# The scan's last product of each state, made by ScalarE and added to y by an accumulating DMA

## The chip, the cores and the metric

The kernel runs on one core of a Trainium2 chip. The metric is the device time in microseconds of one execution; a kernel is compared by the median of its runs. Engines are named as in the profile: PE is TensorE (matrix products and transposes; PEld its weight loads), DVE is VectorE, ACT is ScalarE, POOL is GpSimd, SP is SyncE, which here only issues DMAs.

## The reference

Two layers on x of shape 4 x 64 x 64 x 256, all in float32. The first is a state-space block with a convolution and a feed-forward part, the second is attention over the 4096 pixels of an image. What matters here is the scan in the first layer. Windows of 2 x 2 pixels are sequences of four steps; each of 384 channels has eight states:

```python
dt = silu(dt_raw @ dt_W + dt_b)
dA = exp(dt[..., None] * -exp(A_log))
dBx = dt[..., None] * b_st[:, :, None, :] * x[..., None]
def step(state, inp):
    dA_t, dBx_t, c_t = inp
    state = dA_t * state + dBx_t
    y = einsum('bcn,bn->bc', state, c_t)
    return state, y
...
y_ssm = 0.5 * (y_fwd + y_bwd)          # the scan forwards and backwards over the window
y = alpha * y_ssm + (1 - alpha) * gelu(depthwise_conv(x_proj) @ pw_W)
x_out = x + (y * silu(z)) @ out_W
out1 = x_out + gelu(layernorm(x_out) @ W1 + b1) @ W2 + b2
# second layer: softmax(g f^T) h, times Wo and gamma, plus its input
```

So y at each of the four steps is a sum of eight products, a state times its c, from each direction.

## The kernel before

The first layer goes through 32 blocks (four images, eight blocks each) of 512 pixels. A block's 512 pixels are 128 windows on the partitions times four steps t. Channels-first tiles are [128, 3, 512], and tiles with the windows on the partitions, such as u (dt times x) and y, are [128, 4, 384]: step t, then channels. The second layer, attention, handles 128 queries at a time beside the first layer's later blocks, and 256 queries at a time once the first layer is done.

`scan` handles one block. y starts at t = 0 and 3 with a product by ACT (L438) and one by DVE (L440). Then 25 rounds j follow, in which the forward direction (d = 0) does step j and the backward direction (d = 1) does step j - 1. A step is a pair of state n and position k (j = 3n + k, k = 0, 1, 2), and has these parts:

- `decays` (L406): three ACT exponentials for a direction and state, one state ahead, into a tile e of which there are three.
- `turned` (L462): three PE transposes of a 128-column piece of e into one PSUM bank.
- `decayed` (L470, L474): DVE multiplies the bank with the state before, giving p.
- `carried` (L492): for k < 2, DVE adds the new input to p, giving the state h.
- `given` (L485, or L483 on ACT for two first writes in a block): c times the state is added to y at step t = order[d][k + 1]. For k < 2 the state is h. For k = 2, the last step of the direction, there is no `carried`, and the state is p. For k = 2, t is 3 for d = 0 and 0 for d = 1; no other step of the scan touches y at t = 0 or 3 after L440.

After the scan, `merge` (L562 to L564) transposes y with PE, in the order f, then t = 0, 1, 2, 3, into a bank, and DVE adds it, scaled, to the block's xc.

The program is written as generators, and each engine executes its instructions in the order in which they are written out. A `yield` carries an estimated cost. `first_layer` alternates a block's scan with the pieces of the block before's convolution and `tail` and of the next block's `head` in proportion to these costs. `ensue` puts the next block's `prepare` near the scan's end. Between scan and merge come the rest of the next head's pieces and the next block's `inputs(at + 1, 0)` (L419 to L423). In attention, `fill(RATE)` takes 5.7 cost units of the first layer per step of `attend`.

`layernorm` (L295 to L303), called twice in a block, has DVE statistics, then two small POOL instructions, ve (L300) and rstd (L301), and then four DVE instructions (L303) that need rstd. POOL otherwise adds a bias row (L660), and clears edges (L534, L546) and a column of ones (L700). POOL issues no DMA in this kernel; loads and stores are issued by SP, weights by ACT.

`SLOTS` lists tiles whose memory the late attention uses for its exponentials, and `quarter` loads an image's keys into a tile; `late_weights` calls it for an image that no earlier call has loaded.

Of the kernel before, what the change touches and what calls it, by code (L numbers as in the profile page):

```python
# [21 lines left out]
F32 = mybir.dt.float32  # L22
# [6 lines left out]
P = 128  # L29
DIM = 256  # L30
INNER = 384
# [28 lines left out]
def block_then_attention_kernel(  # L60
# [366 lines left out]
    def scan(at, ensue):  # L427

        bc, cb, dts, es = steps[at]
        if at == 0:  # L430
            yield from inputs(at, 0)
        yield from inputs(at, 1)
        decays(at, 0, 1)
        u = us[at, 0], us[at, 1]
        y = one.tile([P, 4, INNER], F32, tag="y", name="y")

        for t in (0, 3):
            nc.scalar.activation(y[:, t, :], u[0][:, t, :], AF.Copy, scale=cb[:, 2 * t : 2 * t + 1])  # L438
        for t in (0, 3):
            nc.vector.scalar_tensor_tensor(  # L440
                y[:, t, :], u[1][:, t, :], cb[:, 2 * t + 1 : 2 * t + 2], y[:, t, :], ALU.mult, ALU.add
            )
        yield 1.1

        order = ((0, 1, 2, 3), (3, 2, 1, 0))
        hs = {}

        def place(d, j):  # L450

            if at < NBLK and (2 * j + d) % 4 == 3:
                return pso.tile([P, TOK], F32, tag="pso", name="pa")
            return bank()

        def turned(d, j):

            n, k = divmod(j, 3)
            off = (order[d][k + 1] - (1 - d)) * P
            pa = place(d, j)  # L460
            for f in range(KI):
                nc.tensor.transpose(pa[:, f * P : (f + 1) * P], es[d, n][:, f, off : off + P], ident)  # L462
            return pa

        def decayed(d, j, pa):
            n, k = divmod(j, 3)
            t0 = order[d][k]
            p = three.tile([P, INNER], F32, tag="p", name="p")
            if k == 0:
                nc.vector.scalar_tensor_tensor(  # L470
                    p, pa[:, :INNER], bc[:, t0, d, n : n + 1], u[d][:, t0, :], ALU.mult, ALU.mult
                )
            else:
                nc.vector.tensor_tensor(p, pa[:, :INNER], hs[d], ALU.mult)  # L474
            return p

        def given(d, j, p):
            n, k = divmod(j, 3)
            t = order[d][k + 1]
            h = hs[d] if k < 2 else p  # L480
            c = bc[:, t, d, NST + n : NST + n + 1]
            if d == 0 and n == 0 and k < 2:
                nc.scalar.activation(y[:, t, :], h, AF.Copy, scale=c)  # L483
            else:
                nc.vector.scalar_tensor_tensor(y[:, t, :], h, c, y[:, t, :], ALU.mult, ALU.add)  # L485

        def carried(d, j, p):
            n, k = divmod(j, 3)
            if k < 2:
                t = order[d][k + 1]  # L490
                hs[d] = three.tile([P, INNER], F32, tag="h", name="h")
                nc.vector.scalar_tensor_tensor(  # L492
                    hs[d], u[d][:, t, :], bc[:, t, d, n : n + 1], p, ALU.mult, ALU.add
                )


        pas = {(0, 0): turned(0, 0)}
        for j in range(3 * NST + 1):
            n, k = divmod(j, 3)
            first, second = j < 3 * NST, j > 0  # L500
            if k == 2 and n + 1 < NST:
                decays(at, n + 1, 1)
            if first and k == 1 and n + 1 < NST:
                decays(at, n + 1, 0)
            p0 = decayed(0, j, pas.pop((0, j))) if first else None
            p1 = decayed(1, j - 1, pas.pop((1, j - 1))) if second else None
            if first:
                carried(0, j, p0)
                if j + 1 < 3 * NST:
                    pas[0, j + 1] = turned(0, j + 1)  # L510
                pas[1, j] = turned(1, j)
                yield 1.3
            if second:
                carried(1, j - 1, p1)
            if first:
                given(0, j, p0)
            if second:
                given(1, j - 1, p1)
            yield 2.0
            if j == 3 * NST - 4:  # L520
                ensue = ensue()
            if j >= 3 * NST - 4:
                for cost in ensue:
                    yield cost
                    if j < 3 * NST and cost > 2.0:
                        break
        merged[at] = y
# [27 lines left out]
    def merge(at):  # L555

        y = merged.pop(at)
        xc = heads[at][1]
        for f in range(KI):
            py = bank()  # L560
            for t in range(4):
                nc.tensor.transpose(py[:, t * P : (t + 1) * P], y[:, t, f * P : (f + 1) * P], ident)  # L562
            nc.scalar.activation(xc[:, f, :], xc[:, f, :], AF.Copy, scale=half_d[:, f : f + 1])
            nc.vector.scalar_tensor_tensor(xc[:, f, :], py, half_a[:, f : f + 1], xc[:, f, :], ALU.mult, ALU.add)  # L564
            yield 1.1
# [237 lines left out]
    def quarter(b, pool, tag):  # L803

        fQ = pool.tile([P, N // 4], F32, tag=tag, name="fQ")
        for i in range(NBLK):
            nc.sync.dma_start(
                out=fQ[CK * (i % 4) : CK * (i % 4 + 1), (i // 4) * TOK : (i // 4 + 1) * TOK],
                in_=fgd[b * NBLK + i][:CK, :],
            )  # L810
        quarters[b] = fQ
# [81 lines left out]
    def until(at):  # L893
# [2 lines left out]


    SLOTS = (
        (three, "xc"), (three, "e"), (two, "u"), (two, "dt"), (one, "y"), (one, "yz"), (three, "xc"), (three, "e"),
        (three, "xc"), (three, "e"), (two, "u"), (two, "dt"), (two, "xnT"), (two, "xnT"), (one, "ff"), (one, "zs"),  # L900
    )

# [20 lines left out]
    def late_weights(b, q, odd, es):  # L923


        if b not in quarters:
            quarter(b, one, "norm" if b % 2 else "xo")
        fQ, gq = quarters[b], gqs.pop((b, q))
        mx = two.tile([P, 2, QB], F32, tag="uT", name="mx")
        for g in range(4):  # L930
            pr = four()
            for s in range(2):
                at = (g // 2) * TOK + (2 * (g % 2) + s) * P
                for r in range(4):
                    nc.tensor.matmul(  # L935
                        pr[r][:, s * QB : (s + 1) * QB], lhsT=fQ[CK * r : CK * (r + 1), at : at + P],
                        rhs=gq[CK * r : CK * (r + 1), :], start=True, stop=True,
                    )
            for a in range(2):
                pool, tag = SLOTS[8 * odd + 2 * g + a]  # L940
                e = pool.tile([P, 2, 2, QB], F32, tag=tag, name="eT")
                for j in range(2):
                    nc.scalar.copy(e[:, j], pr[2 * a + j].rearrange("p (s q) -> p s q", s=2))  # L943
                if g == 0 and a == 0:
                    nc.vector.tensor_tensor(mx, e[:, 0], e[:, 1], ALU.max)
                else:
                    for j in range(2):
                        nc.vector.tensor_tensor(mx, mx, e[:, j], ALU.max)  # L948
                es.append(e)
                yield  # L950
        yield
        yield
        both = one.tile([P, 2, QB], F32, tag="mx", name="m2")
        m2, nb = both[:, 0, :], both[:, 1, :]
        nc.vector.tensor_tensor(m2, mx[:, 0, :], mx[:, 1, :], ALU.max)
        pm = aside()
        for c in range(2):
            nc.tensor.transpose(pm[:, c * P : (c + 1) * P], m2[:, c * P : (c + 1) * P], ident)
        nm = st.tile([P, 2], F32, tag="nm", name="nm")
        nc.vector.tensor_reduce(  # L960
            nm, pm[:, :QB].rearrange("p (c k) -> p c k", c=2), AX.X, ALU.max, negate=True
        )
        wide = three.tile([P, 2, P], F32, tag="p", name="nmb")
        for c in range(2):
            nc.vector.tensor_copy(wide[:, c, :], nm[:, c : c + 1].to_broadcast([P, P]))
        yield
        pn = aside()
        for c in range(2):
            nc.tensor.transpose(pn[:, c * P : (c + 1) * P], wide[:, c, :], ident)
        nc.scalar.copy(nb, pn[:, :QB])  # L970
        for n, e in enumerate(es):
            e4 = e.rearrange("p r s q -> p (r s) q")
            nc.vector.tensor_tensor(e4, e4, nb.unsqueeze(1).broadcast_to([P, 4, QB]), ALU.add)
            nc.scalar.activation(e, e, AF.Exp)
            if n % 2:
                yield
# [213 lines left out]
```

## Time and profile before

| | |
|---|---|
| median of 3 runs | 5246.53 us (5246.45 to 5246.89) |
| profiled execution, span from first to last instruction | 5245.1 us; the page gives it no other time, and the median lies 1.4 us above |
| instructions | 77394 |
| ACT busy | 3582.8 us, 68% |
| POOL busy | 208.3 us, 4% |
| DMA | 592.13 MB, mean 113 GB/s |
| mean granted PE clock | 0.972 |

Busy times are the sums of an engine's instruction times, overlaps counted once. In a row of the groups, the two numbers after the bar are the busy time of the group in microseconds and the mean duration of one instruction in nanoseconds; after the second bar stands the time that the engine was idle just before these instructions, and what ended it. A row of the waits has the waiting instruction, what it waited for, and then the total in microseconds, the number of times and the longest wait. Matmuls are pipelined, so a group's durations overlap, and the distance between starts tells the cost of one.

### The profile page before, as it was taken

The numbers are of one execution on the slowest core, as the hardware profiler recorded it, in microseconds if no ns is written. First come the engines' busy times: TensorE is split into PE (matmuls) and PEld (weight loads), VectorE is DVE, ScalarE is ACT, GpSimd is POOL, SyncE is SP. The second block draws the span as 40 slices with busy tenths as digits, with TensorE's granted clock in tenths as the row PEclk, the third lists the DMA queues.
The fourth block names the chain that finished last, engine by engine and source line by source line (L and its number), as shares of the span: only waits on it lengthen the run. The fifth ranks groups of instructions, "written<-read, shape, count | busy, mean of one in ns | idle before, by whom it ended". The sixth has DMA issues, their size and how long they took to land. (4 is left out here: it accounts for less than half of the span.)

```text
span 5245.1 us, 77394 instructions
## 1 busy us (share of the span) xinstructions
PE 4861.3 (93%) x27444; PEld 3509.2 (67%) x27444; DVE 4585.4 (87%) x8391; ACT 3582.8 (68%) x5508; POOL 208.3 (4%) x304
## 2 busy tenths in 40 slices
PE   7999998899999999999899999999999889899999
PEld 4565565666666666666666666666666666678887
DVE  7999999889989989988999988899889898866665
ACT  6778778667776767766676766777676767455554
POOL 0000000000000000000000000000000000000000
PEclk8999999999999999999999999999999999999999
DMA  1010011344444434444434444444444344344444
GB/s 48 26 44 19 23 34 36 119 127 126 135 128 135 129 122 122 131 127 124 134 119 127 131 124 127 122 134 128 130 131 131 115 129 130 121 146 147 148 146 139
DMA packets 355779, 592.13 MB, mean 113 GB/s; under 512 B 55104, under 2 KB 95296, under 8 KB 355392
## 3 DMA queue, kind: packets, MB, share of 16 engines
q1 hardware_dynamic: 351872, 583.31, 36.7%
q8 instruction: 217, 3.56, 0.3%
q10 hardware_dynamic: 3520, 3.87, 0.2%
q14 instruction: 170, 1.39, 0.1%
HBM read 528.18 MB, written 58.79 MB: 112 GB/s over the span
## 5 line engine op out<-in xcount | busy, mean ns | idle before, releaser
L1039 PE MATMUL acc<-vt,eq 128*128 128x257 f32 x5888 | 1521.2, 394 | 41.3 <-issue 19.3
L1039 PEld LDWEIGHTS acc<-vt,eq 128*128 128x128 f32 x5888 | 1090.2, 196 | 296.9 <-issue 130.7
L406 ACT ACTIVATE e<-dt,a_sc 128x384 f32<-128x384 f32 x1536 | 853.0, 611 | 250.0 <-PE bank L462 239.7
L462 PE MATMUL bank<-ident,e 128*128 128x128 f32 x4320 | 662.1, 280 | 105.9 <-DVE p L474 59.1
L462 PEld LDWEIGHTS bank<-ident,e 128*128 128x128 f32 x4320 | 523.4, 143 | 329.4 <-issue 94.3
L492 DVE SCALAR_TENSOR_TENSOR h<-u,bc,p 128x384 f32<-128x384 f32 x1024 | 613.1, 611 | 0.1
L852 ACT COPY eq<-q 128x512 f32<-128x512 f32 x736 | 386.1, 588 | 306.7 <-PE q L844 191.4
L485 DVE SCALAR_TENSOR_TENSOR y<-h,bc,y 128x384 f32<-128x384 f32 x960 | 589.4, 614 | 3.6 <-ACT y L483 1.3
L474 DVE TENSOR_TENSOR p<-bank,h 128x384 f32<-128x384 f32 x960 | 515.5, 547 | 49.1 <-PE bank L462 48.4
L878 ACT ACTIVATE eq<-eq 128x1024 f32<-128x1024 f32 x368 | 383.2, 1052 | 145.1 <-DVE eq L877 142.7
L877 DVE TENSOR_TENSOR eq<-eq,nb 128x1024 f32<-128x1024 f32 x368 | 443.6, 1217 | 23.0 <-ACT nb L873 22.6
L595 DVE SCALAR_TENSOR_TENSOR ydw<-xp,vec,ydw 128x512 f32<-128x512 f32 x640 | 462.8, 742 | 0.4
L1014 PE MATMUL bank<-vt,eT 128*128 128x257 f32 x1728 | 432.3, 382 | 0.0
L860 DVE TENSOR_TENSOR mx<-mx,eq 128x512 f32<-128x512 f32 x552 | 382.5, 693 | 52.7 <-ACT eq L852 45.2
L1014 PEld LDWEIGHTS bank<-vt,eT 128*128 128x128 f32 x1728 | 323.4, 189 | 55.6 <-issue 8.6
L485 DVE SCALAR_TENSOR_TENSOR y<-p,bc,y 128x384 f32<-128x384 f32 x512 | 314.0, 613 | 0.1
L626 PE MATMUL q<-ydw,wpw 128*128 128x512 f32 x576 | 282.8, 625 | 30.9 <-ACT eq L852 18.1
L470 DVE SCALAR_TENSOR_TENSOR p<-bank,bc,u 128x384 f32<-128x384 f32 x480 | 291.5, 607 | 17.4 <-PE bank L462 17.0
L406 ACT ACT_TABLE_LOAD x225 | 288.7, 1283 | 10.8 <-PE bank L462 7.0
L844 PE MATMUL q<-gq,fQ 32*128 32x128 f32 x5888 | 246.8, 293 | 35.5 <-ACT eq L852 17.5
L844 PEld LDWEIGHTS q<-gq,fQ 32*128 32x128 f32 x5888 | 202.6, 194 | 105.4 <-ACT eq L852 26.9
L948 DVE TENSOR_TENSOR mx<-mx,eT 128x512 f32<-128x512 f32 x252 | 174.4, 692 | 95.5 <-ACT eT L943 74.8
(153 smaller groups left out, 7021.0 us busy)
## 6 DMA issues: line engine op xcount, KB each, us to landing
vt<-vod SPq DMA_DIRECT2D x1760, 257.0 KB, 2.8
vod<-vst SPq DMA_DIRECT2D x32, 514.0 KB, 4.1
xt<-in_x_dram SPq DMA_DIRECT2D x256, 64.0 KB, 1.9
xo<-in_x_dram SPq DMA_DIRECT2D x256, 64.0 KB, 2.6
x1d<-xo SPq DMA_DIRECT2D x32, 512.0 KB, 2.9
res<-x1d SPq DMA_DIRECT2D x92, 128.0 KB, 2.8
out_dram<-res SPq DMA_DIRECT2D x368, 32.0 KB, 1.6
fgd<-fg SPq DMA_DIRECT2D x32, 256.0 KB, 2.1
```

What stands on the lines that cost most here:

```text
L406: nc.scalar.activation(e[:, f, :], dts[d][:, f, lo : lo + 3 * P], AF.Exp, scale=a_sc[:, d, f * NST + n : f * NST + n + 1],)
L462: nc.tensor.transpose(pa[:, f * P : (f + 1) * P], es[d, n][:, f, off : off + P], ident)
L474: nc.vector.tensor_tensor(p, pa[:, :INNER], hs[d], ALU.mult)
L485: nc.vector.scalar_tensor_tensor(y[:, t, :], h, c, y[:, t, :], ALU.mult, ALU.add)
L492: nc.vector.scalar_tensor_tensor(hs[d], u[d][:, t, :], bc[:, t, d, n : n + 1], p, ALU.mult, ALU.add)
L595: nc.vector.scalar_tensor_tensor(o, x_tap, w_tap, o, ALU.mult, ALU.add)
L844: ins = nc.tensor.matmul(pr[r][:, s * P : (s + 1) * P], lhsT=fQ[CK * r : CK * (r + 1), at : at + P], rhs=gq[CK * r : CK * (r + 1), :], sta ...
L852: nc.scalar.copy(e[:, j, :], pr[2 * a + j])
L877: nc.vector.tensor_tensor(e8, e8, nb.unsqueeze(1).broadcast_to([P, 8, P]), ALU.add)
L878: nc.scalar.activation(e, e, AF.Exp)
L1014: nc.tensor.matmul(sums[c][:, : DIM + 1], lhsT=e[:, r % 2, s, c * P : (c + 1) * P], rhs=vt[:, s, :], start=(n == 0 and s == 0), stop=(n == ...
L1039: nc.tensor.matmul(acc[:, : DIM + 1], lhsT=es[k // 2][:, k % 2, a : a + P], rhs=vt[:, s, :], start=(n == 0 and s == 0), stop=(n == 2 * NI ...
```

## The change

For k = 2, `given` no longer uses DVE. ACT multiplies p by c into a new tile q (128 x 384, of which there are two), and a DMA issued by POOL adds q to y at step t in SBUF. y becomes four tiles, one for each t, where it was one tile; the other uses of y are rewritten for that. The late attention uses the memory of the tile xo where it used y's, and `quarter` always uses the memory tag "norm" for an image that late attention loads.

```diff
-        y = one.tile([P, 4, INNER], F32, tag="y", name="y")
+        y = [one.tile([P, INNER], F32, tag=f"y{t}", name=f"y{t}") for t in range(4)]
...
             c = bc[:, t, d, NST + n : NST + n + 1]
-            if d == 0 and n == 0 and k < 2:
-                nc.scalar.activation(y[:, t, :], h, AF.Copy, scale=c)
+            if k == 2:
+                q = two.tile([P, INNER], F32, tag="q", name="q")
+                nc.scalar.activation(q, h, AF.Copy, scale=c)
+                nc.gpsimd.dma_start(out=y[t], in_=q, accum_op=ALU.add)
+            elif d == 0 and n == 0:
+                nc.scalar.activation(y[t], h, AF.Copy, scale=c)
             else:
-                nc.vector.scalar_tensor_tensor(y[:, t, :], h, c, y[:, t, :], ALU.mult, ALU.add)
+                nc.vector.scalar_tensor_tensor(y[t], h, c, y[t], ALU.mult, ALU.add)
...
-                nc.tensor.transpose(py[:, t * P : (t + 1) * P], y[:, t, f * P : (f + 1) * P], ident)
+                nc.tensor.transpose(py[:, t * P : (t + 1) * P], y[t][:, f * P : (f + 1) * P], ident)
...
-        (three, "xc"), (three, "e"), (two, "u"), (two, "dt"), (one, "y"), (one, "yz"), (three, "xc"), (three, "e"),
+        (three, "xc"), (three, "e"), (two, "u"), (two, "dt"), (one, "xo"), (one, "yz"), (three, "xc"), (three, "e"),
...
-            quarter(b, one, "norm" if b % 2 else "xo")
+            quarter(b, one, "norm")
```

More of the change, by code (lines that the diff above doesn't have):

```diff
@@ L434, in scan @@
         u = us[at, 0], us[at, 1]
-        y = one.tile([P, 4, INNER], F32, tag="y", name="y")
+        y = [one.tile([P, INNER], F32, tag=f"y{t}", name=f"y{t}") for t in range(4)]
         for t in (0, 3):
-            nc.scalar.activation(y[:, t, :], u[0][:, t, :], AF.Copy, scale=cb[:, 2 * t : 2 * t + 1])
+            nc.scalar.activation(y[t], u[0][:, t, :], AF.Copy, scale=cb[:, 2 * t : 2 * t + 1])
         for t in (0, 3):
             nc.vector.scalar_tensor_tensor(
-                y[:, t, :], u[1][:, t, :], cb[:, 2 * t + 1 : 2 * t + 2], y[:, t, :], ALU.mult, ALU.add
+                y[t], u[1][:, t, :], cb[:, 2 * t + 1 : 2 * t + 2], y[t], ALU.mult, ALU.add
             )
```

## The prediction

> **What bounds the kernel now.** I read the page's busy times first, then the windows, because one average hides three stages: scan and convolution blocks alone (to about 920 us), the same blocks beside attention (to about 4540), attention alone.
>
> ```profile
> PE 4861.3 (93%) x27444; PEld 3509.2 (67%) x27444; DVE 4585.4 (87%) x8391; ACT 3582.8 (68%) x5508; POOL 208.3 (4%) x304
> ```
>
> The busy time by stage, in windows that leave out the seams (columns: length, then busy us and instruction count per engine, granted clock, DMA share, GB/s):
>
> ```profile
> 122.00:786.00 664.00, 632.86 (x2771) 392.40 (x2770) 648.51 (x1310) 514.54 (x823) 43.42 (x64) 0.99 0.09 29
> 931.00:4540.00 3609.00, 3316.63 (x19764) 2428.26 (x19763) 3257.03 (x5950) 2536.11 (x3881) 147.05 (x209) 0.97 0.42 127
> 4600.00:5245.00 645.00, 637.36 (x3687) 518.45 (x3685) 401.11 (x573) 316.52 (x464) 0.11 (x1) 1.00 0.49 146
> ```
>
> In the first stage DVE is busy 648.5 of 664 us (98%): it is the bound. One block takes 94.8 us, the distance of one merge (L562) from the next. In the mixed stage PE and DVE are both near 90%, a block takes about 160 us, and neither is the bound alone. The last stage has no scan: nothing happens to it.
>
> What DVE waits for in the mixed stage (us in total, times, longest):
>
> ```profile
> DVE mx L858 <- ACT eq L852: 48.5, 25, 3.6
> DVE p L474 <- PE bank L462: 48.4, 37, 3.7
> DVE mx L860 <- ACT eq L852: 45.2, 32, 4.5
> DVE xt L303 <- POOL rstd L301: 28.8, 20, 1.5
> ```
>
> It waits on PE, ACT and POOL in turns, so a DVE instruction taken away is not given back whole there. PE busy counts pipelined ends; the last chain piece runs 128 matmuls of 257 columns in 27.78 us, 0.844 ns a column. Summing the columns of the matmul records at that pitch (row-packed ones shared out), PE needs about 0.90 of the first stage and 0.83 of the mixed one. So there is room behind DVE, but little in the first stage.
>
> **What is removed.** The groups:
>
> ```profile
> L485 DVE SCALAR_TENSOR_TENSOR y<-p,bc,y 128x384 f32<-128x384 f32 x512 | 314.0, 613 | 0.1
> L483 ACT ACTIVATE y<-h,bc 128x384 f32<-128x384 f32 x64 | 39.2, 613 | 31.0 <-DVE h L492 30.8
> L301 POOL TENSOR_TENSOR rstd<-ve,mhalf 128x4 f32<-128x4 f32 x64 | 67.9, 1061 | 5.3
> L300 POOL TENSOR_SCALAR ve<-mv 128x4 f32<-128x4 f32 x64 | 26.3, 410 | 3566.8 <-DVE mv L297 3401.2 <-DVE rg L983 165.6
> ```
>
> The first row is exactly what goes: 32 blocks x 8 states x 2 directions = 512. Their cost to DVE is the pitch, not the 613 ns, because starts overlap ends (DVE timeline; start, duration):
>
> ```profile
> 441.24 0.61 DVE L485 SCALAR_TENSOR_TENSOR y<-p,bc,y 128x384 f32<-128x384 f32 x1
> 441.76 0.61 DVE L485 SCALAR_TENSOR_TENSOR y<-h,bc,y 128x384 f32<-128x384 f32 x1
> 442.29 0.61 DVE L470 SCALAR_TENSOR_TENSOR p<-bank,bc,u 128x384 f32<-128x384 f32 x1
> ```
>
> So 0.527 us each: 512 x 0.527 = 270 us, 8.4 us a block; 67 in the first eight blocks, 202 in the other 24. How much reaches the end lies between nothing and all. First stage: per 94.8 us DVE falls from 92.9 to 84.5, below PE's 85; the floor is then PE and I take half, 34 us. Mixed stage: DVE falls from 90% to 85%, level with PE's 83% (0.97 clock); I take half, 101. Gain 135.
>
> **What is added on ACT.** 512 scaled copies of L483's form: 613 ns, pitch 0.51, so 261 us; ACT goes from 77% to 86% in the first stage and from 70% to 75.5% in the mixed one. It is off the path where ACT runs ahead; where it is late, PE and DVE already wait (DVE 115 us on ACT's eq and nb copies, PE about 70, in the mixed stage). I raise those 185 by 5.4/70: 14 us. Behind the waiting copy in ACT's queue stand exponentials and attention's evacuations. In 217 places (seven per block) I compared the end of the exponentials that will stand ahead of the copy with the start of the L485 it replaces: ACT is ahead in 120, by 1.9 us on the mean of all, and late in 97, by 0.87. Waiting while ahead costs nothing unless PE is already short of banks; cover gone, 1.9 x 512 = 970 us of waiting at most, of which I take none.
>
> **What is added on POOL and the queues.** 512 DMA issues stand in POOL's queue, each waiting for ACT's copy and for the accumulate before it into the same y. The trace has no DMA issued from POOL. Its time on POOL: 0.1 us (a small memset) to 1.75 (the largest POOL instruction, L272); I take 1.06, the rstd row. Landing, from the DMA rows (KB, median us):
>
> ```profile
> vt<-vod SPq DMA_DIRECT2D x1760, 257.0 KB, 2.8
> vod<-vst SPq DMA_DIRECT2D x32, 514.0 KB, 4.1
> ```
>
> out_dram's 32 KB takes 1.6; with 192 KB I take 2.8, ends 1.6 and 4.1. The path is SBUF to SBUF with an add, which no row has. From the time L485 could start: 0.87 + 0.61 + 1.06 + 2.8 = 5.34 us. Nothing in the scan reads y[0] or y[3] between steps, and accumulates into one tile are three steps (over 10 us) apart, so order and the two q buffers cost nothing; without that gap each step would wait a landing. None of these additions can be a gain. SP's queue is passed by nothing. The DMA engines gain 101 MB, some 17% on 592; at 42% busy the vt loads, issued four ahead, hide it.
>
> The Trainium skill, "SBUF — State Buffer", section "Who interferes with whom", speaks against this: a DMA issued from GpSimd has its descriptors written by GpSimd, which cannot do so while VectorE runs a two-port mode; it names 620 ns growing to 3100. In this trace the scan's DVE instructions take 547 to 613 ns for 384 elements, over one cycle each at the page "VectorE: DVE Perf Modes"'s 0.96 GHz, and only L589 (512 elements, 478 ns, 80 times) looks faster. By the page's worst case, an estimate, each landing would come 2.5 us later, the merges would wait 41 us more by the sums below, and the time would be 5208; by the trace's rows it is the 5167 below, which I keep.
>
> **Where it is waited for.** (1) merge transposes y[0] first. Last L485 of a block, and the merge:
>
> ```profile
> 403.22 0.60 DVE L485 SCALAR_TENSOR_TENSOR y<-p,bc,y 128x384 f32<-128x384 f32 x1
> ```
> ```profile
> 406.85 1.63 PE L562 MATMUL bank<-ident,y 128*128 128x128 f32 x12
> ```
>
> That is 3.6 us in six of the first eight blocks, and 0.7 to 9.6 in the others. Summing what 5.34 exceeds it by: 13.6 us in the first eight, 36.7 in the rest. Behind PE's wait stand the convolution and attention matmuls. I count the first in full, the second half: 32. (2) layernorm's ve and rstd queue behind a DMA on POOL, and DVE waits for rstd in order. The distance from the start of the latest y<-p to ve is under 0.87 + 0.61 + 1.06 = 2.54 us in 7 of 64 layernorms; summing what it lacks: 9. With 1.75 us on POOL, (1) and (2) give 42 and 15.
>
> The y split, the SLOTS name and quarter's tag cost nothing: only batch 3 calls quarter late, with "norm" already, and xo's last readers end before late attention starts.
>
> Sum: -135 + 14 + 32 + 9 = -80 against the span 5245.1; the runs' median lies 1.4 above it. 5246.5 - 80 = 5166.5, say 5167.
>
> **Rivals.** *POOL's issue is slow (slower).* Place: POOL's in-order queue; if one issue holds POOL 4.5 us, ve waits about 80 us over the 64 layernorms (64 at 4 us, 97 at 5), the first merges 41 and half of the other merges' 101, with ACT's 14 that is 186 against 135: 5297. It decides from about 3.5 us (the same sums give 114 at 3, 160 at 4). For it: nothing in the trace bounds a POOL-issued DMA; against it: rows up to 1.75. *The saved DVE time is not on the path (no change).* A fifth of 270 returns, 54, against 55 added: 5246. For it: PE's 0.90 and the mixed waits; against it: DVE's 98% and PE's own waits for DVE p at L462, 76 us in the mixed stage. *More than half returns.* Three quarters, 202, less 40: 5085.
>
> **How the numbers follow.** A measurement tells about 0.2%, 10 us, from no change. Forecast, with the third rival on its side: 0.59 faster (0.49 and 0.10). No change 0.08. POOL slow, and any dearer landing: 0.33. Both signs hold much, so the range runs 5085 to 5300; the forecast's own is 5110 to 5220.
>
> **What would show it.** DVE busy down by about 300 (314 less overlaps), L485 only 960, ACT up by about 310, block distance near 90.5 in the first stage and near 157 in the mixed one, PE waiting for a DMA on y ahead of L562 about 50 us. I am wrong if rstd waits at L303 grow from 60 us towards 150, if POOL's DMA rows exceed 3.5 us, or if DVE's idle grows by all that was removed.

## The result

The changed kernel takes 5262.44 us (median of 6 runs, 5251.62 to 5271.21) beside 5246.49 us for the kernel before: a ratio of 1.0029, 95% interval 1.0018 to 1.0041. It is 16 us slower, where 80 us faster was forecast. The profiled execution, with a span of 5249.8 us, is the fastest of the six, which follow the granted clock (5251.6 us at 0.975, 5271.2 at 0.970), so its trace shows less of the loss, 4.7 us, than the medians do.

The work moved as the change says. The busy times on the page after:

```profile
PE 4854.9 (92%) x27444; PEld 3511.3 (67%) x27444; DVE 4356.6 (83%) x7879; ACT 3821.6 (73%) x6011; POOL 649.4 (12%) x816
```

DVE has 512 instructions and 229 us less, ACT 239 us more, POOL 441 us more. The same windows as before the change, first stage and mixed stage:

```profile
122.00:786.00 664.00, 628.50 (x2732) 388.48 (x2731) 589.93 (x1188) 554.22 (x916) 139.44 (x174) 0.99 0.29 62
931.00:4540.00 3609.00, 3311.59 (x19773) 2428.64 (x19772) 3096.51 (x5584) 2716.99 (x4250) 458.55 (x571) 0.97 0.55 147
```

In the first stage DVE falls from 648.5 to 589.9 us of 664, 98% to 89%, and PE from 632.9 to 628.5: neither of the two is busier (ACT is, 554.2 us for 514.5), and yet a block takes 96.6 us from merge to merge, not 94.8. In the mixed stage a block takes 159.0 us (159.2 before; mean of 23). DVE's time was taken away, and DVE idles instead. What it waits for in the whole run:

```profile
DVE p L474 <- PE bank L462: 89.5, 59, 5.5
DVE mx L864 <- ACT eq L856: 70.6, 51, 3.8
DVE xc L568 <- PE bank L566: 55.3, 23, 5.0
DVE xt L303 <- POOL rstd L301: 46.7, 32, 1.5
```

The first two are waits of before that grew (L474, and L860 there). The third is merge (L564 before, 4.8 us then). The new work itself, in the groups and the DMA issues:

```profile
L484 ACT ACTIVATE q<-p,bc 128x384 f32<-128x384 f32 x512 | 308.9, 609 | 114.2 <-DVE p L474 64.6 <-issue 41.5 <-ACT e L406 5.5
L485 POOL DMA_DIRECT2D y<-q x512 | 445.6, 890 | 3262.7 <-ACT q L484 2925.1 <-PE acc L1043 84.8 <-ACT xp L540 49.6
```
```profile
y<-q POOLq DMA_DIRECT2D x512, 192.0 KB, 3.5
```

One issue holds POOL 0.89 us on the mean, and the data has landed 3.5 us after the issue began (median). Now the end of one first-stage block, engine by engine (start, duration): DVE's last p, ACT up to its last copy, POOL's last issue, PE's transposes of y, DVE's merge.

```profile
399.41 0.55 DVE L474 TENSOR_TENSOR p<-pa,h 128x384 f32<-128x384 f32 x1
```
```profile
399.69 0.61 ACT L406 ACTIVATE e<-dt,a_sc 128x384 f32<-128x384 f32 x1
400.32 1.28 ACT L346 ACT_TABLE_LOAD   x1
401.62 0.69 ACT L346 ACTIVATE zs<-q,b_in 128x512 f32<-128x512 f32 x1
402.32 1.28 ACT L406 ACT_TABLE_LOAD   x1
403.62 0.61 ACT L406 ACTIVATE e<-dt,a_sc 128x384 f32<-128x384 f32 x1
404.14 0.60 ACT L484 ACTIVATE q<-p,bc 128x384 f32<-128x384 f32 x1
```
```profile
405.03 0.86 POOL L485 DMA_DIRECT2D y<-q  x1 [5.51 <-ACT q L484]
```
```profile
408.12 1.50 PE L566 MATMUL bank<-ident,y 128*128 128x128 f32 x12 [0.84 <-DMA y<-q]
```
```profile
408.79 2.07 DVE L568 SCALAR_TENSOR_TENSOR xc<-bank,half_a,xc 128x512 f32<-128x512 f32 x3 [4.92 <-PE bank L566]
```

The last p was ready at 399.96, but ACT came to its copy only 4.2 us later: two exponentials, a silu of the gate (L346) and the two table loads around it stood ahead. PE reaches merge 8.2 us after p, where before it took 3.6 us from the start of the last L485. PE itself idles only 0.84 us, because fourteen convolution matmuls were put ahead. DVE idles 4.92 us, and about as long in five of the six middle blocks of the stage.

### The profile page after: what moved, and what is told of

Read it like the earlier page. It is cut to its first block, busy times and chain, and to the rows that moved or that the text cites. A ratio compares the mean times of both kernels' runs of the same rounds, so it can differ in the third digit from the quotient of the medians.

```text
span 5249.8 us, 78912 instructions
## 1 busy us (share of the span) xinstructions
PE 4854.9 (92%) x27444; PEld 3511.3 (67%) x27444; DVE 4356.6 (83%) x7879; ACT 3821.6 (73%) x6011; POOL 649.4 (12%) x816
## 3 DMA queue, kind: packets, MB, share of 16 engines
q1 hardware_dynamic: 351872, 583.31, 36.8%
q0 software_dynamic: 73728, 100.70, 11.9%
## 5 line engine op out<-in xcount | busy, mean ns | idle before, releaser
L485 POOL DMA_DIRECT2D y<-q x512 | 445.6, 890 | 3262.7 <-ACT q L484 2925.1
L474 DVE TENSOR_TENSOR p<-bank,h 128x384 f32<-128x384 f32 x960 | 519.6, 553 | 91.6 <-PE bank L462 89.5
L484 ACT ACTIVATE q<-p,bc 128x384 f32<-128x384 f32 x512 | 308.9, 609 | 114.2 <-DVE p L474 64.6
L630 PE MATMUL q<-ydw,wpw 128*128 128x512 f32 x576 | 273.0, 608 | 34.5 <-ACT eq L856 28.3
```

What stands on the lines that cost most here:

```text
L485: nc.gpsimd.dma_start(out=y[t], in_=q, accum_op=ALU.add)
```

## Experiments

Each run is compared with runs of the kernel before made beside it: median 5245.08 us for e1 to e4, 5240.58 for e5 to e8, 5239.22 for e9 to e12. Differences below are against these. Theory W was: the gain is there, and waits at a block's end eat it. Its rival P: the gain was never there.

**e1: only the split of y.**

```diff
-            if k == 2:
-                q = two.tile([P, INNER], F32, tag="q", name="q")
-                nc.scalar.activation(q, h, AF.Copy, scale=c)
-                nc.gpsimd.dma_start(out=y[t], in_=q, accum_op=ALU.add)
-            elif d == 0 and n == 0:
+            if d == 0 and n == 0 and k < 2:
```

> y in four tiles and the late tags moved, and the scan's last product on DVE as before. Theory W (the gain is eaten by new waits at a block's end: ACT's copy late, DMA landing, DVE held at merge): 5246, within 5. Theory P (DVE's time isn't what the span is made of; PE with its weight loads and the order of work set it): also about 5246. Theory O (every edit makes the engines' orders anew, and that alone moves the time): off by 10 to 30 us either way.

Measured 5244.12 us, ratio 1.0 (0.999 to 1.0009). The four tiles and the late attention's tags cost nothing. Theory O is not tested by this run, although it was meant to be: every edit lets the planner order the engines' instructions anew, but here PE's, DVE's and POOL's orders came out the same as before in every place, by the names in the trace.

**e2: the product left out.**

```diff
             if k == 2:
-                q = two.tile([P, INNER], F32, tag="q", name="q")
-                nc.scalar.activation(q, h, AF.Copy, scale=c)
-                nc.gpsimd.dma_start(out=y[t], in_=q, accum_op=ALU.add)
+                pass
```

> The last product of each direction (512 products) is left out altogether: no DVE, no ACT, no DMA for it. This is what 270 us of DVE time are worth with nothing put in their place. W: 5246 - 135 = 5111 (5070 to 5150), the first stage's block from 94.8 to about 90.5 us. P: 5225 to 5250, the block near 94 us.

Measured 5166.67 us, ratio 0.9852 (0.9837 to 0.9866): 78 us. So both theories miss: the gain that could be had is neither 135 nor nothing. Most of it, 67 us in the traces, lies in the mixed stage, where a block falls from 159.2 to 156.2 us: 2.9 of the 8.4 us that were taken from DVE. The first stage's block stays at 94.6. The window of its six middle blocks (columns as above), before and in this run:

```profile
218.00:784.00 566.00, 541.23 (x2372) 334.82 (x2372) 553.36 (x1118) 439.33 (x704) 37.26 (x55) 1.00 0.09 28
```
```profile
218.00:784.00 566.00, 541.09 (x2372) 336.00 (x2371) 514.21 (x1028) 440.43 (x707) 37.27 (x56) 0.99 0.09 28
```

DVE is busy 39 us less and every other engine does the same work in the same time. The first block is different: its merge comes 8.4 us earlier than before (113.3 for 121.7 us), all that was taken from DVE there. In its scan PE had room, being busy 61 of 76 us, where DVE was busy 72 (the kernel before):

```profile
44.00:120.00 76.00, 60.91 (x227) 33.85 (x227) 72.07 (x143) 51.84 (x84) 0.00 (x0) 0.77 0.03 8
```

**e3: ACT's copies, without the DMA** (q is added to nothing).

```diff
                 nc.scalar.activation(q, h, AF.Copy, scale=c)
-                nc.gpsimd.dma_start(out=y[t], in_=q, accum_op=ALU.add)
```

> ACT makes q as in the changed kernel, but q is added to nothing: no DMA. W: 14 us above the run that leaves the product out altogether, so 5125 (5085 to 5165). P, with ACT as the cause: within 10 of the changed kernel, 5250 to 5265. The difference to the run without ACT's copies is ACT's price, the difference to the changed kernel is the DMA's.

Measured 5200.51 us, ratio 0.9917 (0.9902 to 0.9932): 45 us below before, so ACT's copies cost 34 us, not 14, and the DMA the other 61 (to 16 above). A block is 95.6 us in the first stage and 157.1 in the mixed one, 1.0 and 0.9 above e2. In this trace the clock granted in the first stage's middle blocks was 0.98, in e2's 0.99, so the 1.0 is not cleanly ACT's.

**e4: the last state on DVE.**

```diff
-            if k == 2:
+            if k == 2 and n + 1 < NST:
...
-            elif d == 0 and n == 0:
+            elif d == 0 and n == 0 and k < 2:
```

> As the changed kernel, but the last state's product (n = 7) of both directions stays on DVE, so nothing that merge waits for comes by DMA late: 448 products by ACT and DMA, 64 on DVE. W: DVE's wait of about 5 us at merge in the first stage goes, and half of the others': 5190 to 5215. P: 5250 to 5262, like the changed kernel.

Measured 5229.55 us, ratio 0.9968 (0.9957 to 0.9979). With the complete result it beats both kernels: 15.5 us below before, 31 below the changed kernel. It lies between the two theories, which e2 explains: the gain W counted on is smaller. DVE's wait at merge:

```profile
L568 DVE SCALAR_TENSOR_TENSOR xc<-bank,half_a,xc 128x512 f32<-128x512 f32 x96 | 67.8, 747 | 5.6 <-PE bank L566 5.2
```

**e5: the product left out, and three taps of the first stage's convolution from PE to DVE** (ACT loses its copy of that channel group with them, 0.59 us a block).

```diff
-        yield from depthwise(ydw, (9, 9, 0) if b == 0 else (0, 0, 0))
+        yield from depthwise(ydw, (9, 6, 0) if b == 0 else (0, 0, 0))
```

> The product left out altogether as in e2 (5166.7), and in the first stage three of the second channel group's nine convolution taps moved from PE to DVE: PE has 2.6 us less a block, DVE 2.0 more. Theory P1 (in the first stage PE is the bound, although DVE is busy 98% there before): the first stage's block falls from 94.6 to about 92.5, 5150 to 5158. Theory S (a chain of waits through all engines sets the block): 94 to 96, 5160 to 5175.

Measured 5137.75 us, ratio 0.9801 (0.9786 to 0.9816): 103 us below before, 24 more than e2. The first stage's block falls to 92.2 us, by 2.4 of the 2.6 us taken from PE, although DVE got 2.0 more:

```profile
218.00:784.00 566.00, 539.24 (x2392) 337.43 (x2391) 535.67 (x1070) 454.74 (x719) 37.56 (x56) 0.99 0.09 28
```

With DVE relieved, PE sets the first stage. By the traces 15 us of the gain over e2 lie there; another 9 came in the mixed stage, whose work is that of e2 but whose granted clock was 0.978, not 0.972.

**e6: the last state's accumulates into a tile of their own** (y lacks these).

```diff
+    aside_y = wp.tile([P, INNER], F32, name="aside_y")
+    nc.gpsimd.memset(aside_y, 0.0)
...
-                nc.gpsimd.dma_start(out=y[t], in_=q, accum_op=ALU.add)
+                nc.gpsimd.dma_start(out=y[t] if n + 1 < NST else aside_y, in_=q, accum_op=ALU.add)
```

> ACT and DMA work exactly as in the changed kernel, but the last state's 64 accumulates go into a tile of their own that nobody reads (so y lacks these), and merge waits for no late DMA. Theory W (the landing that merge waits for is the larger part of the DMA's 62 us): 5262 - 38 = 5224 (5215 to 5232). Theory C (the DMAs cost by POOL's time, the port or the traffic, wherever they land): 5250 to 5262.

Measured 5208.72 us, ratio 0.9937 (0.9922 to 0.9952): 32 below before, where the changed kernel is 16 above. ACT, POOL and DMA work is the same (but for one small memset), so what merge waits for is 48 us. The other DMAs, with their 448 issues and landings, cost 13 us over e3, within the two intervals; PE's order is the same in e3 and in this run.

**e7: ACT's copies made from u instead of p** (and added to nothing).

```diff
-                nc.scalar.activation(q, h, AF.Copy, scale=c)
-                nc.gpsimd.dma_start(out=y[t], in_=q, accum_op=ALU.add)
+                nc.scalar.activation(q, u[d][:, t, :], AF.Copy, scale=c)
```

> ACT's 512 copies as in e3 (5200.5), but made from u, which is long there, in place of p, and added to nothing. Theory B (ACT's price of 34 us is its occupancy, 0.51 us each): 5193 to 5205. Theory F (the price is ACT waiting for p, and what stands behind it): 5167 to 5180.

Measured 5207.08 us, ratio 0.9934 (0.9917 to 0.995): not faster than e3. ACT idled 108.5 us ahead of its copies in e3 and 0.3 us here, so its price is not the wait for p but the time of the copies among ACT's other work. The traces show where that time is waited for: PE's waits that ended on ACT add up to 138 us in e2, 172 in e3 and 187 here, and most of the growth is behind attention's emptying of a PSUM tile (PE q <- ACT eq: 78, 102 and 108).

**e8: e4 only from block 8 on.**

```diff
-            if k == 2:
+            if k == 2 and n + 1 < NST and at >= NBLK:
...
-            elif d == 0 and n == 0:
+            elif d == 0 and n == 0 and k < 2:
```

> As e4 (last state on DVE; 5229.6), and only from block 8 on; the first eight blocks as before. The complete result. Theory P1 (in the first stage the saved DVE time is worth nothing, and ACT and DMA cost 0.8 us a block there): 5219 to 5225. If the first stage's change did help: 5230 to 5240.

Measured 5228.05 us, ratio 0.9976 (0.9967 to 0.9986), 12.5 below before; e4 was 15.5 below. The first stage's block is 94.7 us again (95.6 in e4), but the mixed one is 158.5 (158.2), and no difference remains that these intervals can tell.

**e9: the kernel before, with the taps moved alone** (the edit of e5).

> The kernel before with only the three taps moved from PE to DVE in the first stage (2.6 us less on PE, 2.0 more on DVE a block). If PE alone is the bound there: the block falls from 94.8 to about 92.5, 5222 to 5230. If both PE and DVE bind, which e2 and e5 together suggest: the block rises to 95.5 to 97, 5245 to 5260.

Measured 5260.80 us, ratio 1.0042 (1.0027 to 1.0057): 22 us slower, a block 96.6 us, 1.8 longer for 2.0 us more on DVE.

```profile
218.00:784.00 566.00, 529.72 (x2293) 327.11 (x2291) 551.87 (x1111) 425.65 (x684) 37.28 (x55) 0.98 0.09 28
```

So in the first stage of before DVE, busy 97.5% here, sets the block as well: more DVE work lengthens it at nearly the full price, and less DVE work doesn't shorten it (e2). The two bound it at almost the same length. That less PE work helps only once DVE has room fits this run but isn't shown by it alone: at a granted clock of 0.98, where before had 1.00, PE was busy 90.9 us a block, as long as before (90.6). By the traces 12 of the 22 us came up to the eighth merge; the rest came later, where the work is that of before.

**e10: e4 with the taps moved** (the edits of e4 and e5).

> e4 (last state's product on DVE, the other 448 by ACT and DMA) with the three taps moved as in e5. The complete result. Both bind in the first stage: e4's 0.9968 of the kernel before less about 27 us, 5195 to 5212, the first stage's block near 93. ACT or POOL binds there by now: 5222 to 5235.

Measured 5210.72 us, ratio 0.9946 (0.9932 to 0.9961): with the complete result the best of all, 28.5 us below before. The first stage's block is 93.3 us, as expected; the mixed one is 158.8, 0.6 above e4's, which keeps the sum at the upper end.

**e11: the last state at high priority in the planner.**

```diff
-                nc.scalar.activation(q, h, AF.Copy, scale=c)
-                nc.gpsimd.dma_start(out=y[t], in_=q, accum_op=ALU.add)
+                with tc.high_priority() if n + 1 == NST else nullcontext():
+                    nc.scalar.activation(q, h, AF.Copy, scale=c)
+                    nc.gpsimd.dma_start(out=y[t], in_=q, accum_op=ALU.add)
```

> The changed kernel with the last state's copies and accumulates at high priority in the planner that orders the engines' work. The complete result. Theory W (ACT reaches the last copy 4.2 us late in the first stage, 1.7 in the mixed one, and DVE waits for what follows at merge): DVE's wait at merge falls from 54 to about 20 us, 5230 to 5245. If ACT's place is not moved by it: 5255 to 5265.

Measured 5247.54 us, ratio 1.0009 (0.9999 to 1.002). ACT now reaches the last copy 0.9 us after p in the first eight blocks (4.2 in the changed kernel) and 0.6 in the others (1.7). DVE's idle time at merge (L569) is 34.5 us, not 20:

```profile
L569 DVE SCALAR_TENSOR_TENSOR xc<-bank,half_a,xc 128x512 f32<-128x512 f32 x96 | 67.4, 745 | 34.5 <-PE bank L567 34.0
```

The first stage's block falls to 95.1, but the mixed one is 159.5. An earlier place in ACT's order takes away 21 of the 55 us of DVE's wait; what stays, against 5.6 in e4, goes with the copy, the issue and the landing. The whole run is 8 us above before, the changed kernel 16, and the two intervals touch.

**e12: e2 with less PE work in the mixed stage** (one of three partial products of the pointwise convolution left out from block 8 on, beside e2's product).

```diff
+            nk = KI if b == 0 else KI - 1
-            for k in range(KI):
+            for k in range(nk):
...
-                    start=(k == 0), stop=(k == KI - 1),
+                    start=(k == 0), stop=(k == nk - 1),
```

> The product left out as in e2, and from block 8 on one of the three partial products of the pointwise convolution is left out too: PE has 2.6 us less a block there, 61 us in all, and nothing else changes. If PE binds the mixed stage for the part that DVE doesn't (DVE gave back 3.0 of 8.4 us a block): 30 to 45 us below e2. If PE is no bound there: within 8 of e2 (0.985 of the kernel before).

Measured 5113.37 us, ratio 0.976 (0.9745 to 0.9775): 126 below before, 47.5 more than e2, for 61 us of PE time: 78% comes back, against 29% of DVE's 270 in e2 (2.9 of 8.4 us a block in the mixed stage alone). With DVE relieved, PE is what most of the mixed stage is made of. A little of it may be the clock (0.975 granted in the mixed stage, 0.972 in e2), and no run took PE work away there with DVE's left as before.

## Why the prediction was wrong

Its sum was -135 + 14 + 32 + 9 = -80. The runs give -78 (e2), +34 (e3 less e2), +48 (changed kernel less e6) and +13 (e6 less e3): +17. But for rounding they must add up to the measured 16, as each is the difference to the next run. Of the 97 us between the two sums, 57 are gain that did not come, 20 are ACT's, 16 merge's and 4 the last term's.

**The step that failed first is "I take half".** The count of 512 and the pitch of 0.527 us were right, and so was the note that part of 270 us is not given back. But the first stage was read as "DVE is busy 98%: it is the bound", with PE's need put at 0.90 by its pitch, and 34 us were counted there. e2 shows 11.5 by the eighth merge, 8.4 of them in the first block, and next to nothing in the middle ones: 94.8 to 94.6. PE's busy time in that window, 541 of 566 us in both runs, was the sign that I argued away as pipelined ends; e5 shows that it was real. In the mixed stage 101 was taken and 67 came. What stands in its place is PE (e5, e12). The traces agree: PE's waits that ended on DVE add up to 222 us in the kernel before and to 143 in e2, a fall of 79 beside a gain of 78 (its waits on ACT rose by 19, its busy time fell by 21). The 222 stood in the trace ahead of the change, against the 270 that the sum started from.

**ACT's 14 was 34.** I scaled the waits that already ended on ACT by its added share. This leaves out that a copy of 0.51 us also delays the evacuations behind it that PE waits for: PE's waits that ended on ACT grew by 35 us from e2 to e3. DVE's waits for ACT, most of what I had scaled, are no measure of it. The two mx rows (L858 and L860 before) add up to 94 us before, to 121 in e2, where ACT makes no copies, and to 128 in e3, so most of their growth comes with the relieved DVE and not with ACT's copies.

**Merge's 32 was 48, and fell on another engine.** The landing was put 5.34 us after p; it is 8.3 us in the first eight blocks and 7.3 in the others, means over all blocks, until PE's transposes. Issue and landing were about right: 1.06 + 2.8 = 3.86 us were put, and from the start of a block's last issue to its landing it is 3.1 us in the first eight blocks and 4.1 in the others. The largest miss is ACT's lag behind p: 0.87 was put, and at a block's end it is 4.2 us in the first eight blocks and 1.7 in the others. In the block shown above, a silu of the gate with its two table loads is most of it. The 0.87 was a mean over 217 steps, seven in a block; over the other 480 copies of the changed kernel the lag is 2.0 us on the mean and 0.9 at the median. I expected PE to wait "about 50 us"; PE's own waits for the DMA are 29.7 us, and DVE's idle time at merge is 55.3.

**The 9 us for rstd were about nothing.** DVE's waits at L303 rose from 60.4 to 74.3 us, but in e2, where POOL issues no DMA, they are 72.1: it is the relieved DVE that comes earlier. e6's 13 us for all DMAs but the last stand in its place, little above the runs' spread.

**The rivals.** "The saved DVE time is not on the path" was the nearest: 54 of gain against 55 of cost, where it was 78 against 95. Of the signs of being wrong the last one came: DVE's busy time fell by 229 us and its idle time grew by 234. The slow rival had its mechanism wrong: POOL's issue is 0.89 us, far under the 3.5 from which it was to decide. The Trainium skill, "SBUF — State Buffer", section "Who interferes with whom", would have a POOL issue wait while VectorE runs a two-port instruction. No run here shows a delay like the one that the prediction priced at 2.5 us: the median of 512 issues is 859 ns and the longest 1245, with DVE busy 83% of the span. The 42 issues that overlap a TENSOR_SCALAR of DVE (L303, or L593, the L589 of before) have a median of 923 ns, the other 470 of 859.

A statement ahead of the prediction is wrong, too: instructions are not issued in the order in which they are written out. The planner orders each engine's instructions by its own estimates, keeps dependencies, and starts over with every edit. With the product left out nothing that PE does was changed, and yet its order differs from that of the kernel before in 2859 of 27444 places; with y split alone, in none. So no run shows what a new order costs by itself, and a part of a difference between two runs may be that. The nearest is e11, which changes only priorities and moves the time by some 8 us against the changed kernel, far less than the terms of 78, 34 and 48 us.

## What to carry to other kernels

An engine that is busy 98% of a stage is not proof that the stage shortens with it: leave the work out, with nothing in its place, and measure; if PE stands at 95% beside it, as in this first stage, expect to gain only when both are relieved (e2 nothing in the middle blocks, e5 2.4 us a block, e9 1.8 us the wrong way). Work moved to a DMA is paid for where its last result is read: keep the last step of a chain on the engine that the reader follows, and move only steps whose result has time (e4: 31 us better than moving all). And take the lag of the engine that must feed such a step from that very place, not from the mean of the loop.

## What the runs showed of the hardware that was not expected

- A POOL-issued accumulating DMA of 192 KB, SBUF to SBUF, holds POOL 0.86 us and lands 3.5 us after the issue begins (medians). Byte for byte it takes about twice the DMA time of SP's loads and stores: 100.70 MB took 11.9% of the 16 engines' span, 583.31 MB took 36.8%. The vt loads beside it landed in 2.9 us, 2.8 before.

```profile
q1 hardware_dynamic: 351872, 583.31, 36.8%
q0 software_dynamic: 73728, 100.70, 11.9%
```

- DVE hardly notices: L492's mean duration is 611 ns before, 615 in e2 without any DMA, and 619 with the 512 of them.
